# A graph-network kernel: its first block prepared in another order, a shorter lag between its layers, and its last block updated in halves

## Chip, cores, metric

One core of one Trainium2 chip. The metric is device time in microseconds, the median of several executions; before and after were timed on the same chip in the same rounds. Ratios are the mean time of one kernel's fast runs over that of the other's of the same rounds, so not quite the ratio of the medians quoted. "Span" is the length of the one profiled execution; times in traces count from its start. In the rounds of the experiments the kernel before took 653.9 to 655.2 us (medians), 3 to 5 us more than in those of the result, so kernels of different rounds are compared by their ratios or traces.

## The reference, cut

128 graphs of 64 nodes with 128 features. For each pair of nodes a message network runs on the concatenated features; messages are masked by the adjacency matrix, summed over neighbours, and an update network of the same form is added to the features.

```python
def _mlp(x, w0, b0, g0, be0, w1, b1, g1, be1, w2, b2):
    h = jax.nn.relu(x @ w0 + b0)
    h = _layernorm(h, g0, be0)
    h = jax.nn.relu(h @ w1 + b1)
    h = _layernorm(h, g1, be1)
    return h @ w2 + b2

messages = _mlp(pair_feats, msg_w0, ...) * coupling_matrix[..., None]
agg = jnp.sum(messages, axis=2)
updated = part_feats + _mlp(jnp.concatenate([part_feats, agg], -1), upd_w0, ...)
```

## The kernel before

Some names first: two graphs are a pair (128 nodes), two pairs a quad (2560 edge places, five iterations, `QC`), two quads a block. The rows of layer 0 are products of node features and weights; marks and compares build the matrix that picks two rows for each edge. A root is the standard deviation that a layer norm divides by. PSUM is the memory that TensorE writes to; a bank is one buffer of a pool in it, and this kernel's pools have eight.

It lists the edges that exist, 640 places for a graph, and works on 160 iterations of 512 edges. Iteration n runs layer 0 of edges n, layer 1 of edges n - 10, and, on a plan of (iteration, place in it, function), everything else: 16 blocks of 8 graphs are prepared, reduced and updated, one block every ten iterations (`CPB = 10`). Each engine is given its instructions in the order in which the plan emits them, and the traces show them start in that order (under e6_bias a ReLU whose input TensorE ends at 22.00 us starts at 25.12, after the pack of the bias table that the plan puts before it). All eight banks are in use; the update layers, the rows of layer 0 and the derived weights share one (`ps_u`), the transposes two (`ps_a`):

```python
ps_a = es.enter_context(tc.tile_pool(name="ps_a", bufs=2, space=PSUM))
ps_u = es.enter_context(tc.tile_pool(name="ps_u", bufs=1, space=PSUM))
...
def ubank():
    return ps_u.tile([P, 512], F32, name="mu")
...
def layer(b, *pairs):
    ps = ubank()
    ...                       # 8 or 16 passes of TensorE into ps
...
L1 = 2 * QC                   # lag of layer 1: QC = 5
for b in range(NB):
    o = b * CPB
    ...
    u = o + L1 + 3 * QC
    ...
    at(u + 6, "x", lambda b: layer(b, ("xnT", u0a), ("ysumT", W["w2u"])), b)
    at(u + 7, "m", layer_out, b, "uh", "m0")        # DVE empties the bank
    ...
    at(u + 11, "x", lambda b: layer(b, ("uhT", W["u1c"])), b)
    at(u + 12, "m", layer_out, b, "uy", "usdb")     # DVE
    ...
    at(u + 17, "x", lambda b: layer(b, ("uyT", W["u2c"])), b)
    at(u + 18, "m", finish, b)                      # DVE, then the store
...
for n in range(last + 1):
    run(n, "a"); run(n, "m")
    if 0 <= n - L1 < NCHK: layer1(n - L1)
    if n < NCHK: layer0(n)
    ...                       # transposes, statistics, marks and compares
    for k in ("x", "x1", "x2", "e1", "e"):
        run(n, k)
```

A block's first and last update layer stand at u + 6 and u + 17, eleven iterations apart, and the next block's u is ten higher. The last layer of a block therefore runs one iteration after the first layer of the next, whose result DVE has taken by then.

Of the kernel before, what the change touches and what calls it, by code (L numbers as in the profile page):

```python
# [23 lines left out]
def tile_gnn(  # L24
# [74 lines left out]

    an0 = const.tile([P, 2, PB, N], F32, name="an0")  # L100
    xn0 = const.tile([P, 2, PB, C], F32, name="xn0")

    def load_first(b):
        nc.sync.dma_start(an0[:, b], adjp[:, b * PB:(b + 1) * PB, :])
        nc.sync.dma_start(xn0[:, b], xf[b * PB * P:(b + 1) * PB * P, :]
                          .rearrange("(q p) c -> p q c", p=P))

    load_first(0)
    w0a = mat(mw0[0:C, :], "w0a")
    w0b = mat(mw0[C:2 * C, :], "w0b")  # L110
    b0c = col(mb0, "b0c")
    load_first(1)
# [16 lines left out]

    eps_c = const.tile([P, 1], F32, name="eps_c")  # L130
# [3 lines left out]
    nc.scalar.activation(eps2_c, eps_c, AF.Square)  # L134
    first = const.tile([P, PB, N], F32, name="first")
# [5 lines left out]
    lt = const.tile([P, P], F32, name="lt")  # L141
    nc.vector.memset(lt, 1.0)
    nc.gpsimd.affine_select(out=lt, in_=lt, pattern=[[1, P]], compare_op=ALU.is_ge,
                            fill=0.0, base=0, channel_multiplier=-1)
    nc.vector.memset(lt[0:N, N:P], 0.0)

# [3 lines left out]
    nc.vector.memset(dq[N:N + 1, N - 1:N], 0.0)  # L150
# [5 lines left out]
    nc.vector.memset(pick32[0:N, N:N + 1], 0.0)  # L156
    pick = const.tile([P, 2, N], F16, name="pick")
    nc.vector.tensor_copy(pick.rearrange("p g m -> p (g m)"), pick32)
# [4 lines left out]
    cmpt = const.tile([P, 4 * CAP], F16, name="cmpt")  # L163
    ones_row = const.tile([1, P], F32, name="ones_row")
    nc.vector.memset(ones_row, 1.0)
    mean_m = const.tile([P, P], F32, name="mean_m")
    nc.vector.memset(mean_m, 1.0 / C)
# [77 lines left out]
    def square_sum(stp, st, n, name):  # L245

        d = stp.tile([P, n], F32, name=name + "_d")
        s = stp.tile([P, n], F32, name=name + "_s")
        m2 = stp.tile([P, n], F32, name=name)
        nc.gpsimd.tensor_tensor(d, st[:, :, 1], st[:, :, 4], op=ALU.subtract)  # L250
        nc.gpsimd.tensor_tensor(s, st[:, :, 2], st[:, :, 5], op=ALU.add)
        nc.gpsimd.tensor_tensor(d, d, d, op=ALU.mult)
        nc.gpsimd.tensor_scalar(d, d, C / 4.0, None, op0=ALU.mult)
        nc.gpsimd.tensor_tensor(m2, d, s, op=ALU.add)
        return m2
# [7 lines left out]
    def var1_of(stp, st, m20, n, name):  # L263

        v = stp.tile([P, n], F32, name=name + "_v")
        nc.gpsimd.tensor_scalar(v, m20, EPS, None, op0=ALU.mult)
        m2 = square_sum(stp, st, n, name)
        nc.gpsimd.tensor_tensor(v, v, m2, op=ALU.add)
        return v
# [20 lines left out]
    def edge_path(es):  # L290
# [5 lines left out]
        hp = es.enter_context(tc.tile_pool(name="hp", bufs=11))  # L296
        yp = es.enter_context(tc.tile_pool(name="yp", bufs=14))
# [66 lines left out]
        def count_out(b):  # L364
            blk = blocks[b]
            nc.scalar.copy(cumall[:, b * PB:(b + 1) * PB], blk.pop("ps")[:, 0:PB])
            blk["deg"] = blkp.tile([P, PB], F32, name="deg", bufs=5)
            nc.scalar.copy(blk["deg"], blk["rk"][:, :, N - 1])

        def place(b):  # L370

            blk = blocks[b]
            an = blk.pop("an")
# [6 lines left out]
            nc.gpsimd.tensor_tensor(pos, pos, an, op=ALU.mult)  # L380
            blk["pos"] = pos
            qs = qsp.tile([P, PB, 2, P], F16, name="qs")
            nc.gpsimd.tensor_copy(qs[:, :, :, 0:N],
                                  pick.unsqueeze(1).to_broadcast([P, PB, 2, N]))
            nc.gpsimd.memset(qs[N:P, :, 0, N:P], 0.0)
            nc.gpsimd.memset(qs[0:N, :, 1, N:P], 0.0)
            blk["qs"] = qs

            a2 = adp.tile([P, PB, N], F32, name="a2")
            nc.gpsimd.tensor_tensor(a2, an, an, op=ALU.mult)  # L390
            nc.gpsimd.tensor_tensor(a2, a2, an, op=ALU.subtract)
            blk["a2"] = a2
# [19 lines left out]
        def turn(b, src):  # L412
            blk = blocks[b]
            blk[src + "_ps"] = abank()
            for q in range(PB):
                nc.tensor.transpose(blk[src + "_ps"][:, q * P:(q + 1) * P], blk[src][:, q, :],
                                    ident)

        def turn_out(b, src, bufs=1):
            blk = blocks[b]  # L420
            blk[src + "T"] = blkp.tile([P, PB * P], F32, name=src + "T", bufs=bufs)
            nc.scalar.copy(blk[src + "T"], blk.pop(src + "_ps"))
# [77 lines left out]

        def var0_of(q):
            V0[q] = square_sum(stp, ST0.pop(q), QT, "m20")
# [40 lines left out]
        def var1_step(q):  # L543
            Q[q] = var1_of(stp, ST1.pop(q), V0.pop(q), QT, "m21")

        def bias_table():
# [23 lines left out]
            nc.gpsimd.tensor_tensor(W["b1t"], mix[0:K].unsqueeze(1).to_broadcast([K, QT, C]),  # L570
                                    tile_of[0:K].unsqueeze(2).to_broadcast([K, QT, C]),
                                    op=ALU.mult)
# [26 lines left out]
        def weights(p):  # L599
# [3 lines left out]
            for g in range(2):  # L603
                k = (2 * h + g) * TG
                nc.gpsimd.tensor_tensor(  # L605
                    w[:, :, g, :], OH[p][:, :, g, :],
                    Q[q][:, k:k + TG].unsqueeze(2).to_broadcast([P, TG, N]), op=ALU.mult)
# [3 lines left out]
        def reduce(p):  # L611
            b, k = divmod(p, PB)
            if k == 0:
# [13 lines left out]
        def sums_out(b):  # L627
            blocks[b]["ysum"] = updp.tile([P, PB, C], F32, name="ysum")
            nc.scalar.copy(blocks[b]["ysum"], YS.pop(b))

        def bias0(b):
            m0 = updp.tile([P, PB, C], F32, name="m0")
            nc.gpsimd.tensor_tensor(
                m0, bc(W["c2u"], PB),
                blocks[b]["deg"].unsqueeze(2).to_broadcast([P, PB, C]), op=ALU.mult)
            nc.gpsimd.tensor_tensor(m0, m0, bc(W["ub0b"], PB), op=ALU.add)
            blocks[b]["m0"] = m0

        def residual(b):
            xo = updp.tile([P, PB, C], F32, name="xo")  # L640
            nc.gpsimd.tensor_tensor(xo, blocks[b]["xn"], bc(W["cu2b"], PB), op=ALU.add)
            blocks[b]["xo"] = xo

        def layer(b, *pairs):
            ps = ubank()
            for q in range(PB):
                s = slice(q * P, (q + 1) * P)
                for n, (src, w) in enumerate(pairs):
                    nc.tensor.matmul(ps[:, s], lhsT=blocks[b][src][:, s], rhs=w, start=(n == 0),
                                     stop=(n == len(pairs) - 1))  # L650
            blocks[b]["l_ps"] = ps.rearrange("p (q c) -> p q c", q=PB)

        def layer_out(b, o, bias):
            t = updp.tile([P, PB, C], F32, name=o)
            add_relu(t, blocks[b]["l_ps"], blocks[b][bias])
            blocks[b][o] = t
            st = updp.tile([P, PB, 6], F32, name=o + "_st")
            for q in range(PB):
                nc.vector.bn_stats(st[:, q, :], t[:, q, :])
            blocks[b][o + "_st"] = st  # L660

        def upd_m0(b):
            blocks[b]["m2"] = square_sum(updp, blocks[b]["uh_st"], PB, "um0")

        def upd_root0(b):
            blocks[b]["sd"] = root0(updp, blocks[b]["m2"], PB, "um0")

        def upd_shift(b):
            sdb = updp.tile([P, PB, C], F32, name="usdb")
            nc.gpsimd.tensor_tensor(  # L670
                sdb, bc(W["bu1b"], PB),
                blocks[b]["sd"].unsqueeze(2).to_broadcast([P, PB, C]), op=ALU.mult)
            blocks[b]["usdb"] = sdb

        def upd_m1(b):
            blocks[b]["v1"] = var1_of(updp, blocks[b]["uy_st"], blocks[b]["m2"], PB, "um1")

        def upd_root1(b):
            blocks[b]["v1"] = root1(updp, blocks[b]["v1"], PB, "um1")

        def upd_inverse(b):
            blocks[b]["q1"] = inverse(updp, blocks[b]["v1"], PB, "um1")

        def finish(b):
            blk = blocks[b]
            o = updp.tile([P, PB, C], F32, name="uo")
            for q in range(PB):
                nc.vector.scalar_tensor_tensor(o[:, q, :], blk["l_ps"][:, q, :],  # L688
                                               blk["q1"][:, q:q + 1], blk["xo"][:, q, :],
                                               op0=ALU.mult, op1=ALU.add)  # L690
            nc.sync.dma_start(of[b * PB * P:(b + 1) * PB * P, :]
                              .rearrange("(q p) c -> p q c", p=P), o)
            blocks[b] = None
# [6 lines left out]
        L1 = 2 * QC  # L700
        for b in range(NB):
# [4 lines left out]
            if b > 0:  # L706
                r = max(o - 12, 0)
                at(max(o - 13, 0), "m", rank, b)
                at(r, "x", count, b)
                at(r + 1, "a", count_out, b)  # L710
                at(r + 1 if b == 1 else o - 9, "e", place, b)
                at(o - 6, "m", odd_weights, b)
                at(o - 6, "x", steps, b)
                at(o - 5, "a", steps_out, b)
                at(o - 7, "x", turn, b, "xn")
# [296 lines left out]
```

## Time and profile before

| | before |
|---|---|
| time, median of 4 | 650.62 us (650.29 to 653.32) |
| span of the profiled run (an execution of 655.82 us, above the four timed) | 653.6 us |
| TensorE busy, whole span | 624.3 us, 96% |
| TensorE busy, 45.2 to 588.0 us | all of 542.8 us |
| DVE, POOL, ACT busy, whole span | 76%, 58%, 53% |

The prediction shows and reads the lines.

### The profile page before, as it was taken

The page shows a single profiled execution, that of the slowest core. Times are in us where ns is not written, and L with a number is a line of the kernel's source. Part 1 is how long each engine was busy: PE and PEld are TensorE (multiplying, and loading weights), DVE is VectorE, ACT ScalarE, POOL GpSimd, SP SyncE. Part 2 cuts the span into 40 slices and gives each one's busy share as a digit, 9 for nine tenths or more (in the row PEclk, how much of TensorE's full clock was granted, in tenths as well). Part 3 has the DMA queues.
Part 4 walks back from the last instruction along what each step waited for, and adds up shares of the span by engine and source line. Part 5 has one row for each costly group of instructions (what it writes and reads, how often), then busy time and mean ns, then how long its engine had stood idle before and what let it go on. Part 6 is the DMA issues. An engine that isn't in the chain of part 4 may idle for free. (4 is left out here: it accounts for less than half of the span.)

```text
span 653.6 us, 15818 instructions
## 1 busy us (share of the span) xinstructions
PE 624.3 (96%) x5859; PEld 573.4 (88%) x5859; DVE 496.4 (76%) x1871; ACT 349.3 (53%) x788; POOL 377.5 (58%) x956
## 2 busy tenths in 40 slices
PE   4989999999999999999999999999999999999864
PEld 2778999999999999999999999999999999998753
DVE  4778888888777878887777888877787888875332
ACT  2435565665646465665646556565656566464321
POOL 6624446556483846657383855658384765456552
PEclk9979999999999999999999999999999999999985
DMA  4100000001001010101001010100100000000001
GB/s 116 39 1 26 2 25 2 3 1 42 1 3 42 1 42 3 42 2 25 17 3 42 2 43 1 42 2 2 42 1 18 2 18 2 17 3 18 2 17 34
DMA packets 27884, 12.06 MB, mean 18 GB/s; under 512 B 10390, under 2 KB 27804, under 8 KB 27804
## 3 DMA queue, kind: packets, MB, share of 16 engines
q1 hardware_dynamic: 27804, 11.02, 6.4%
q8 instruction: 47, 0.77, 0.5%
q14 instruction: 33, 0.27, 0.1%
HBM read 6.82 MB, written 4.19 MB: 17 GB/s over the span
## 5 line engine op out<-in xcount | busy, mean ns | idle before, releaser
L499 DVE BATCH_NORM_STATS2 st<-hT 128x6 f32<-128x128 f32 x640 | 140.8, 282 | 55.3 <-PE hT L495 55.0
L531 PEld LDWEIGHTS z<-w1c,h 128*128 128x128 f32 x1280 | 168.7, 192 | 7.0
L531 PE MATMUL z<-w1c,h 128*128 128x128 f32 x1280 | 168.9, 275 | 0.0
L541 DVE BATCH_NORM_STATS2 st<-y 128x6 f32<-128x128 f32 x640 | 137.8, 277 | 10.8 <-ACT y L534 10.8
L534 ACT ACTIVATE y<-z 128x512 f32<-128x512 f32 x160 | 95.7, 598 | 87.4 <-PE z L531 86.4
L489 ACT ACTIVATE h<-hps,b0c 128x512 f32<-128x512 f32 x160 | 109.4, 684 | 12.5 <-PE hps L486 12.4
L478 DVE TENSOR_TENSOR s<-mk,cmpt 128x512 fp32r<-128x512 f32 x160 | 107.6, 673 | 4.6 <-POOL cmpt L782 4.0
L495 PE MATMUL hT<-ident,h 128*128 128x128 f32 x640 | 98.1, 276 | 1.7 <-DVE st L499 1.7
L486 PE MATMUL hps<-s,abl 128*128 128x512 f32 (+3 forms) x256 | 93.0, 375 | 0.0
L605 POOL TENSOR_TENSOR w<-oh,m_q 128x320 f32<-128x320 f16 x128 | 89.9, 725 | 3.2 <-PE ma L589 1.0
L495 PEld LDWEIGHTS hT<-ident,h 128*128 128x128 f32 x640 | 76.9, 142 | 12.3 <-DVE st L499 2.4
L596 ACT CAST oh<-ma 128x384 f16<-128x384 f32 (+1 forms) x128 | 48.2, 429 | 61.9 <-PE ma L589 61.1
L528 PE MATMUL z<-b1t,sdT 80*128 80x512 f32 x160 | 78.9, 493 | 1.9 <-ACT y L534 1.9
L620 PE MATMUL ys<-y,w 128*64 128x128 f32 x1280 | 78.2, 275 | 1.0 <-POOL w L605 1.0
L486 PE MATMUL hps<-s,abh 128*128 128x512 f32 (+3 forms) x256 | 79.1, 327 | 0.0
L620 PEld LDWEIGHTS ys<-y,w 128*64 128x64 f32 x1280 | 69.5, 137 | 8.6 <-POOL m_d L250 2.9
L510 POOL TENSOR_TENSOR sh<-m_sd,sh 128x40 fp32r<-128x40 f32 x32 | 8.7, 271 | 116.9 <-ACT sh L509 116.9
L471 PE MATMUL mk<-tp,qs 128*128 128x512 f16 (+3 forms) x256 | 62.2, 305 | 3.9 <-DVE s L478 3.4
L446 DVE TENSOR_TENSOR abl<-mu,abh 128x512 fp32r<-128x512 f32 x32 | 22.1, 691 | 53.2 <-ACT abh L439 53.2
L250 POOL TENSOR_TENSOR m_d<-st 128x20 f32<-128x20 f32 x64 | 16.1, 252 | 79.2 <-DVE st L541 66.9
L486 PEld LDWEIGHTS hps<-s,abl 128*128 128x128 f32 x256 | 49.9, 195 | 0.8 <-issue 0.7
L486 PEld LDWEIGHTS hps<-s,abh 128*128 128x128 f32 x256 | 50.0, 195 | 0.0
(184 smaller groups left out, 1074.8 us busy)
## 6 DMA issues: line engine op xcount, KB each, us to landing
xn<-in_x_dram SPq DMA_DIRECT2D x16, 256.0 KB, 3.5
out_dram<-uo SPq DMA_DIRECT2D x16, 256.0 KB, 2.5
an<-in_adj_dram SPq DMA_DIRECT2D x16, 128.0 KB, 2.6
w<-in_L_gnn_msg_w_dram SPq DMA_DIRECT2D x2, 64.0 KB, 2.7
u<-in_L_gnn_upd_w_dram SPq DMA_DIRECT2D x2, 64.0 KB, 2.1
w0a<-in_L_gnn_msg_w_dram SPq DMA_DIRECT2D x1, 64.0 KB
w0b<-in_L_gnn_msg_w_dram SPq DMA_DIRECT2D x1, 64.0 KB
u0b<-in_L_gnn_upd_w_dram SPq DMA_DIRECT2D x1, 64.0 KB, 1.7
```

What stands on the lines that cost most here:

```text
L471: nc.tensor.matmul(MK[n][:, c:c + w], lhsT=blocks[g // (2 * PB)]["qs"][:, g // 2 % PB, g % 2, :], rhs=TP[g // 2][:, e:e + w], start=True, ...
L478: nc.vector.tensor_tensor(S[n], MK.pop(n), cmpt[:, o:o + CH * P], op=ALU.is_equal)
L486: nc.tensor.matmul(ps[:, c:c + w], lhsT=ab[:, g % 4, :], rhs=s[:, c:c + w], start=(k == 0), stop=(k == 1))
L489: nc.scalar.activation(H[n], ps, AF.Relu, bias=b0c)
L495: nc.tensor.transpose(ps[:, t, :], H[n][:, t * P:(t + 1) * P], ident)
L499: nc.vector.bn_stats(ST0[q][:, CH * c + t, :], ps[:, t, :])
L528: nc.tensor.matmul(ps, lhsT=SD[q], rhs=W["b1t"][:, CH * c:CH * c + CH, :], start=True, stop=False, skip_group_check=True)
L531: nc.tensor.matmul(ps[:, t, :], lhsT=h[:, t * P:(t + 1) * P], rhs=W["w1c"], start=False, stop=True, skip_group_check=True)
L534: nc.scalar.activation(Y[n], ps, AF.Relu)
L541: nc.vector.bn_stats(ST1[q][:, CH * c + t, :], Y[n][:, t, :])
L605: nc.gpsimd.tensor_tensor(w[:, :, g, :], OH[p][:, :, g, :], Q[q][:, k:k + TG].unsqueeze(2).to_broadcast([P, TG, N]), op=ALU.mult)
L620: nc.tensor.matmul(YS[b][g * N:(g + 1) * N, k, :], lhsT=w[:, t, g, :], rhs=y, start=(t == 0), stop=(t == TG - 1))
```

## The change

Its intent: shorten both ends. Four parts, from a long diff:

```diff
 # head: split loads, two weights issued by ACT, TensorE warmed, chain reordered
-    load_first(0)
-    w0a = mat(mw0[0:C, :], "w0a")
+    nc.sync.dma_start(an0[:, 0], adjp[:, 0:PB, :])
+    load_first(0, 0, 2)
+    w0a = mat(mw0[0:C, :], "w0a", nc.scalar)
 ...
+        for n in range(7):
+            nc.tensor.matmul(warm[:, 0:P], lhsT=mean_m, rhs=mean_m, start=True, stop=True)
 ...
-            nc.gpsimd.tensor_tensor(W["b1t"], mix..., tile_of..., op=ALU.mult)
+        def bias_part(c):                              # on ACT, in five packs of four
+            for t in range(CH * c, CH * c + CH):
+                nc.scalar.activation(W["b1t"][:, t, :], W["b1mix"], AF.Copy,
+                                     scale=W["tile_of"][:, t:t + 1])
+        for c in range(QC):
+            at(4 + c, "a", bias_part, c)
 # lag
-        L1 = 2 * QC
+        L1 = QC + 3
+        SC = QC + L1 + QC
 # updates: n is the start of the block's update, one block every ten iterations
-            at(u + 6, "x", lambda b: layer(b, ("xnT", u0a), ("ysumT", W["w2u"])), b)
-            at(u + 17, "x", lambda b: layer(b, ("uyT", W["u2c"])), b)
-            at(u + 18, "m", finish, b)
+                at(n + 3, "x", lambda u: layer(u, ("xn", u0a), ("ysumT", W["w2u"])), u)
+                at(n + 13, "x", lambda u: layer(u, ("uyT", W["u2c"])), u)
+                at(n + 14, "m", finish, u)
 # tail: last block in two halves, its small operations on DVE instead of POOL
+            if b < NB - 1:
+                units = [(Unit(b, 0, PB, nc.gpsimd), o + QC + SC)]
+            else:
+                units = [(Unit(b, 0, 2, nc.vector), o + SC), (Unit(b, 2, 2, nc.vector),
+                                                              o + QC + SC)]
+            return nc.vector if q == NQ - 1 else nc.gpsimd      # last quad's variances
+                (nc.vector if p == NP - 2 else nc.gpsimd).tensor_tensor(   # weights
```

## The prediction

> **What bounds the kernel now.** I read the page's slices first, then the busy time by stretch, then the waits of TensorE alone, then the timelines of the first 60 us and of the last 65 us. The slices say where to look:
>
> ```profile
> PE   4989999999999999999999999999999999999864
> PEclk9979999999999999999999999999999999999985
> ```
>
> TensorE is full except in the first two slices and the last three, and its clock falls only near the third slice and at the end. Busy time by stretch (start and end in us, length, then PE, PEld, DVE, ACT, POOL busy, then the granted clock) shows how sharp that is:
>
> ```profile
> 15.30:20.00 4.70, 4.23 (x24) 2.89 (x23) 2.33 (x4) 0.69 (x1) 2.87 (x7) 1.00 0.71 187
> 33.30:38.10 4.80, 2.65 (x16) 1.62 (x15) 4.80 (x13) 1.12 (x3) 2.81 (x7) 0.96 0.00 0
> 38.10:41.10 3.00, 3.00 (x15) 2.85 (x14) 1.60 (x7) 0.82 (x3) 0.00 (x0) 0.50 0.00 0
> 45.20:588.00 542.80, 542.80 (x5258) 505.24 (x5258) 442.78 (x1688) 315.59 (x711) 317.69 (x819) 1.00 0.06 15
> 588.00:653.60 65.60, 48.71 (x424) 42.59 (x422) 25.13 (x102) 19.13 (x46) 34.73 (x88) 0.83 0.06 17
> ```
>
> From 45.2 to 588.0 us TensorE has no gap at all, with DVE at 82% and POOL at 59%. No part of the change takes work from TensorE, so these 542.8 us cannot shrink; only the head and the tail can. TensorE's own waits (who waited, on whom, us in total, times, longest) lie in those two places too:
>
> ```profile
> PE ma L416 <- DMA xn<-in_x_dram: 4.7, 1, 4.7
> PE mk L471 <- DVE s L478: 3.4, 1, 3.4
> PE mu L649 <- ACT ysumT L422: 2.3, 1, 2.3
> PE hT L495 <- DVE st L499: 1.7, 1, 1.7
> PE ys L620 <- POOL w L605: 1.0, 4, 0.3
> ```
>
> The head's timeline (start, duration) names the causes:
>
> ```profile
> 14.41 0.69 DVE L478 TENSOR_TENSOR s<-mk,cmpt 128x512 fp32r<-128x512 f32 x1 [3.97 <-POOL cmpt L782]
> 15.29 0.88 PE L486 MATMUL hps<-s,abl 128*128 128x512 f32 x1
> 27.25 0.48 PE L486 MATMUL hps<-s,abl 128*128 128x512 f32 x1
> 30.22 4.47 POOL L570 TENSOR_TENSOR b1t<-b1mix,tile_of 80x2560 fp32r<-80x2560 f32 x1
> 32.89 1.99 DVE L455 TENSOR_SCALAR tp<-slot,cumall 128x640 f16<-128x640 f16 x1
> ```
>
> The first compare waits 3.97 us for a table that POOL fills last, so layer 0 starts at 15.29. The same matmul takes 0.88 us there and 0.48 at 27.25: TensorE is at half rate until about 24.2, although the clock column still prints 1.00 (it seems to know no throttle before its first event). Then POOL's bias table holds POOL for 4.47 us; a DVE instruction that takes 0.38 us elsewhere (at 26.02) takes 1.99 beside it and ends with it at 34.9; TensorE stands still, and its clock is 0.50 from 37.8 to 44.6.
>
> The tail's timeline shows a latency chain, not a full engine:
>
> ```profile
> 626.76 1.16 PE L649 MATMUL mu<-u1c,uhT 128*128 128x128 f32 x8
> 632.47 0.80 PE L649 MATMUL mu<-w2u,ysumT 128*128 128x128 f32 x2 [2.35 <-ACT ysumT L422]
> 646.51 2.07 PE L649 MATMUL mu<-u2c,uyT 128*128 128x128 f32 x8 [2.06 <-ACTq L975]
> ```
>
> The last reduction ends at 626.7, and 26.9 us more pass: transposes, three small layers, statistics on POOL and roots on ACT one after another, at half clock from about 632.
>
> [...] 0.88 against 0.48 us, and the fall at 37.8 after the gap of 33.9 to 35.7. [...] TensorE was busy from 18.1 and warm at 24.2. [...] here one issue takes 0.43 to 0.51 us, so moving two weights to ACT is worth about 1 us of issue.
>
> **A ledger of TensorE work at full clock.** From start-to-start times in the full stretch: layer 0 of an iteration 0.55, transposes 0.44, marks 0.25, layer 1 1.20, reduction of two pairs 2.33, node marks 0.25, transposes of a block 0.44, first update layer 1.8, the other two 0.9 each, a half of the rows 1.0. Up to 45.2 us: ten iterations of layer 0 (12.4), rows 3.0, one layer 1 (1.2), preparation and derived weights together about 4.8: 21.4. The head therefore loses 45.2 - 21.4 = 23.8 us. After 588.0: ten layer 1 (12.0), four double reductions (9.3), six node marks (1.5), eight transposes (3.5), layers 5.4 + 2.7 + 3.6, the rest 0.6: 38.6; the tail loses 65.6 - 38.6 = 27.0. Total work 21.4 + 542.8 + 38.6 = 602.8.
>
> **The change part by part: head.** The table is built early and in parts, the step tables are emptied by two engines, the degrees leave the chain, and the placement goes from POOL (0.30 + 0.63 + 0.73) to DVE. New chain: adjacency lands 3.1, scan to 3.8; seven warm-up matmuls, 14 passes of 0.21 us, end about 4.2 and cost the count 0.4; count and copy to 5.0; placement of five DVE instructions to 6.0; meanwhile x's first half turned at 5.5; rows (2.0 us cold) to 7.5; steps to 8.7; copies 0.35, marks 0.6, compare 0.7: layer 0 at about 10.6, against 15.29, so 4.7 earlier. A memset of 1.6 us (three quarters of the 2.19 seen) now sits between the first two compares, so the second iteration starts near 13.5, against 20.0. Iterations 1 and 2 cold at 3.3, iteration 3 with rows 2.5 to 3.5, iteration 4 about 3 (below), 5 to 7 at 2.3, the DVE's load there (0.89 + 0.67 + about 0.7): iteration 8, where layer 1 now starts, comes at 32.5. Work done by then: 15.5. Loss 17.0 in place of 23.8; I take a **gain of 6.4 us**. It includes that the stall behind the bias table, with its cold 7 us, does not come back.
>
> **Lag of 8.** In the full stretch it moves nothing off TensorE. Its worth is at the ends: two iterations fewer with layer 0 alone (where DVE, not TensorE, is the limit), and 7.9 us of work done before layer 0 ends that was done after: two layer 1 (2.4), one double reduction (2.3), two node marks (0.5), the first update layer of one block (1.8) and the last of another (0.9). So 30.7 us of work stays in the tail.
>
> **Tail.** Let T be the end of layer 0. Layer 1 alone is spaced by 2.08 us when nothing fills it (as from 599.77 to 601.85), since one bank of PSUM waits for ACT. Iterations 160 to 167 come to about 20.3 us with one double reduction and the updates between. Reduction of the next pairs and of the last ones, with the last weights split over DVE and POOL and variances on DVE: ends near T + 27. From there the last half's chain: copy 0.4, held about 1 by a root that ACT takes first; turn, copy, first layer with the neighbours' work in the queue to T + 31.5; add, statistics and the small DVE operations (12 of about 0.17 us) 3.5; root 0.3, shift on POOL 0.55, second layer 0.9, add and variance 2.0, root and inverse 0.6, copy and last layer 1.3, finish 0.57, store 3.8 (as 649.8 to 653.6), and about 1.5 for cold matmuls: T + 47. The tail then loses 47 - 30.7 = 16.3 in place of 27.0: a **gain of 10.7 us**.
>
> **Sum.** 6.4 + 10.7 = 17.1 us. Span 653.6 - 17.1 = 636.5; for the time, 650.4 - 17.1 = 633.
>
> **The rivals.** (1) ACT becomes the head's new stop. The bias table is now 20 small activations in four-packs ahead of the ReLU of iterations 4 to 8, and the first pack waits for a POOL chain of 1.7 us after a DVE reduction. In-order ACT then holds the ReLU, and the one bank of layer 0 holds TensorE. I put in 1 us; if it is 3 and the clock drops again, the head gains 2 and the time is 637. For it: ACT sits at its limit nowhere else, but this wait is in program order. (2) The shorter lag exposes the root's chain in every group of five iterations: root, cast, POOL's difference and transpose now stand in one iteration. 0.5 us in each of 32 groups would be 16 us and the time 649. Against it: the transposition is placed last in TensorE's list, behind 0.9 to 3.1 us of update layers, and POOL's weights precede it in another iteration. (3) The halves cost more than they save: small operations have fixed costs (0.16 us for an inverse of 128x4), three units interleave in in-order queues, and tail gains only 4: 640. (4) The warm-up works at once, and the cold stretch of 15 to 24 us goes as well: 3 to 4 us more, 629.
>
> **Range and chances.** (1) and (3) in part are likely, (4) as likely as not, (2) unlikely as a whole. From 626 (both ends better by 3 to 4) to 641 (one rival in full). The line for 2% is 637.4, 4 us above my figure with a spread of about 6: faster 0.77, same 0.22, slower 0.01.
>
> **What would show it.** Right: layer 0's first ReLU at 11 to 13 us instead of 16.63; no gap near 34 and no half clock from 37.8 to 44.6; between the first layer 1 and the end of layer 0 TensorE still without gaps; last reduction's end to the span's end near 20 us instead of 26.9. Wrong: gaps of TensorE that repeat every five iterations, a TensorE wait on ACT in the first 30 us above 2 us, or a chain after the last reduction of over 24 us.

Measured in the trace of before: 0.88 and 0.48 us are the two matmuls above, and the first ten DMA issues take 0.43 to 0.51 us (later ones down to 0.25). The clock column prints 1.00 up to 24.06 us, where the record of the clock begins. For the fixed costs of rival 3: an inverse of 128x4 takes 0.16 us on DVE, one of 128x20, five times as much, 0.26.

## The result

**698.91 us (698.02 to 699.34) against 650.62: ratio 1.0731, interval 1.070 to 1.076.** The change is 7% slower. The span is 696.3 us.

The slices of the changed kernel, to be laid beside those of before:

```profile
PE   6799999899998989989898998989899898989874
PEclk8999999999999999999999999999999999999986
```

The tail looks alike, and the first two slices (6 and 7 in place of 4 and 9) do not tell which head is better; the ruler below does. But the middle, which had no slice under 9, now has an 8 every two or three slices. Busy time by stretch (same columns as in the prediction) says the same:

```profile
100.00:600.00 500.00, 471.70 (x4478) 438.93 (x4477) 369.28 (x1403) 267.45 (x599) 270.79 (x709) 0.97 0.06 15
```

TensorE now stands still for 28.3 of 500 us there, and its granted clock is 0.97. TensorE's waits name one cause (us in total, times, longest):

```profile
PE mu L701 <- DVE uo L737: 34.8, 16, 2.6
PE mu L701 <- ACT uyT L692: 3.6, 2, 2.1
PE ma L538 <- POOL sh L533: 3.2, 4, 1.1
PE hps L505 <- ACT h L508: 2.8, 2, 2.5
PE mk L490 <- DVE s L497: 2.8, 2, 1.9
```

L701 is the update layer and `mu` the bank that `ubank()` hands out; L737 is the finish. Sixteen waits of 2.2 us on average, about one a block. One of them, from the timelines of TensorE and of DVE:

```profile
294.35 1.11 PE L701 MATMUL mu<-u2c,uyT 128*128 128x128 f32 x8
296.67 1.10 DVE L737 SCALAR_TENSOR_TENSOR uo<-mu,um_q,xo 128x128 f32<-128x128 f32 x4
297.82 0.80 PE L701 MATMUL mu<-u0a,xnT 128*128 128x128 f32 x2 [2.36 <-DVE uo L737]
298.41 0.64 PE L701 MATMUL mu<-w2u,ysumT 128*128 128x128 f32 x2
```

The last layer of a block ends at 295.46. The first layer of the next block, in the same iteration, wants the same bank. DVE can empty it only after the rest of its own iteration, at 296.67, and TensorE resumes at 297.82. The last line also shows the second price: the pair takes 0.64 us where it takes 0.39 at full clock (as at 339.56). The granted clock by stretches of 2 us (the third number from the end; the share and rate of DMA follow it) shows how long that lasts:

```profile
296.00:298.00 2.00, 0.18 (x1) 0.18 (x2) 1.77 (x8) 0.00 (x0) 0.08 (x1) 0.93 0.00 0
298.00:300.00 2.00, 2.00 (x10) 2.00 (x11) 0.00 (x0) 0.00 (x0) 0.00 (x0) 0.50 0.63 158
300.00:302.00 2.00, 2.00 (x12) 1.88 (x12) 0.41 (x1) 0.08 (x1) 0.00 (x0) 0.71 0.64 170
302.00:304.00 2.00, 2.00 (x18) 1.95 (x18) 1.15 (x5) 1.76 (x5) 0.65 (x4) 1.00 0.00 0
```

Not every block pays it: after the wait at 336.85 to 339.23 the clock stayed at 1.00. The record of the clock shows a pattern in this. The eight half-clock stretches between 100 and 600 us last 3.41 us each and start whole multiples of 3.41 us apart (174.85, 256.77, 297.73 us and so on). Cut into intervals of the same length, on the same starts, each of them follows an interval in which TensorE stood still for 1.94 to 2.37 us; the four waits that cost no clock left at most 1.84 us in one interval. That holds for 100 to 600 us of this one trace only: after 600 us an interval with 1.91 us of standing still (from 622.00) is followed by full clock, and one with 1.77 us (from 662.96) by half. What decides it is not shown; no run was made to test it.

A ruler for all kernels below is the start of layer 0's ReLU on ACT, of which there is one in each iteration. These numbers come from the timelines (us):

| kernel | iteration 0 | 8 | 28 | 148 | 158 | end of span | 28 to 148 |
|---|---|---|---|---|---|---|---|
| before | 16.63 | 39.45 | 103.31 | 549.08 | 584.52 | 653.6 | 445.8 |
| after | 10.28 | 35.55 | 102.85 | 593.14 | 632.56 | 696.3 | 490.3 |
| e1_later | 10.52 | 36.55 | 103.86 | 550.32 | 589.19 | 644.4 | 446.5 |
| e5_flag | 10.27 | 35.95 | 103.31 | 549.66 | 585.87 | 641.2 | 446.4 |
| e7_all | 12.89 | 34.61 | 101.98 | 548.32 | 584.52 | 639.9 | 446.3 |
| e12_all_again | 10.43 | 32.62 | 100.00 | 546.49 | 582.71 | 638.0 | 446.5 |
| e9_whole | 12.90 | 33.18 | 100.58 | 547.01 | 583.23 | 640.2 | 446.4 |
| e10_pool | 12.91 | 33.14 | 100.51 | 546.96 | 583.19 | 645.6 | 446.5 |
| e11_tailbanks | 10.28 | 32.88 | 100.25 | 546.74 | 582.96 | 636.5 | 446.5 |

From iteration 28 to 148, twelve blocks, the change costs 44.5 us: 3.7 a block, of which about 2.35 is standing still (28.3 us over the twelve waits in 100 to 600 us) and the rest is slower work: for the same 4368 matmuls TensorE is busy 462.0 us, against 446.4 in e1_later below, which fits the stretches at half clock: eight of 3.41 us at 0.50 lose at most 13.7 of these 15.6 us, an estimate.

### The profile page after: what moved, and what is told of

Read it like the earlier page. It is cut to its first block, busy times and chain, and to the rows that moved or that the text cites. A ratio compares the mean times of both kernels' runs of the same rounds, so it can differ in the third digit from the quotient of the medians.

```text
span 696.3 us, 15879 instructions
## 1 busy us (share of the span) xinstructions
PE 636.4 (91%) x5873; PEld 584.2 (84%) x5873; DVE 503.2 (72%) x1917; ACT 359.0 (52%) x814; POOL 361.8 (52%) x932
## 4 chain that ended last, share of the span: by engine, by line
## 5 line engine op out<-in xcount | busy, mean ns | idle before, releaser
L701 PE MATMUL mu<-u0a,xnT 128*128 128x128 f32 x128 | 34.8, 365 | 34.1 <-DVE uo L737 32.6
L701 PEld LDWEIGHTS mu<-u0a,xnT 128*128 128x128 f32 x128 | 26.9, 259 | 37.3 <-DVE uo L737 35.3
L252 POOL TENSOR_TENSOR um_d<-uh_st 128x4 f32<-128x4 f32 x15 | 3.1, 207 | 92.6 <-DVE uh_st L711 92.6
```

Source lines behind the costliest of these rows:

```text
L701: nc.tensor.matmul(ps[:, s], lhsT=l, rhs=w, start=(n == 0), stop=(n == len(pairs) - 1))
```

## The experiments

**Theory A: the bank.** The first layer stands at 3 after a unit's start, the last at 13, and blocks start ten apart: both ask for the one bank in the same iteration. **Theory B: the lag.** The shorter lag exposes the root's chain or makes another engine the bound (rival 2 of the prediction).

### e1_later: the last layer one iteration later

```diff
-                at(n + 13, "x", lambda u: layer(u, ("uyT", W["u2c"])), u)
-                at(n + 14, "m", finish, u)
+                at(n + 14, "x", lambda u: layer(u, ("uyT", W["u2c"])), u)
+                at(n + 15, "m", finish, u)
```

> The changed kernel with the last update layer and the finish of every block one iteration later, nothing else. Theory A (the single PSUM bank that all update layers, rows and derived weights share is asked for by two blocks in one iteration: the last layer of a block stands at 13 after its start, the first layer of the next block at 3 after its own start, and blocks start 10 apart): TensorE's wait on the finish, 34.8 us in 16 times, falls below 4 us, ten iterations take about 36.5 us again instead of 41.5, and the time is 638 to 646. Theory B (the shorter lag exposes the root's chain, or ACT or POOL became the bound): nothing changes by more than 5 us, so 694 to 704.

Measured: 646.81 us against 654.80 of before, ratio 0.990. TensorE in the middle:

```profile
100.00:570.00 470.00, 469.95 (x4610) 439.56 (x4610) 381.72 (x1457) 275.57 (x616) 279.90 (x735) 1.00 0.06 16
```

No idle time, full clock, 446.5 us for twelve blocks as before (445.8). Two numbers undo the whole loss and leave a small gain; the lag of 8 costs next to nothing in the middle. The time is 0.8 us above the range expected.

### e2_otherbank: nothing moved, another bank

```diff
         def layer(u, *pairs):
-            ps = ubank()
+            ps = abank() if pairs[0][0] == "uyT" else ubank()
```

> The changed kernel with every instruction in its place, but the last update layer writes to the pool of two PSUM banks that transposes use, in place of the single bank. Theory A: the wait on the finish goes although nothing moved in the schedule; 638 to 650, the slack for the bank of the transposes being unknown. Theory B, or a theory that the place of the layer in the order is what hurts and not the bank: 694 to 704.

Measured: 651.30 us, ratio 0.996 (0.992 to 1.000). The order of instructions is that of the slow kernel, only the bank differs, and the loss is gone: 1.073 has become 0.996, and iterations 28 to 148 take 451.3 us instead of 490.3. Of the 4.8 us that are left there against e1_later, 2.7 are new small waits on the transposes' banks:

```profile
PE ma L538 <- DVE uo L737: 2.7, 11, 0.2
```

The other 2.1 are busy time and were not traced. So it is the bank and not the place. The time is 1.3 us above the range I had given.

### e3_before_collide: the collision alone, in the kernel before

```diff
-            at(u + 17, "x", lambda b: layer(b, ("uyT", W["u2c"])), b)
-            at(u + 18, "m", finish, b)
+            at(u + 16, "x", lambda b: layer(b, ("uyT", W["u2c"])), b)
+            at(u + 17, "m", finish, b)
```

> The kernel before, with its last update layer and finish one iteration earlier, so that last layer and next block's first layer stand in one iteration there too; none of the change is in it. Theory A: about 2.4 us of wait and 1 to 2 us of slow clock per block for 15 blocks, so 690 to 705 instead of 650. Theory B: 648 to 653.

Measured: 708.61 us against 654.80, ratio 1.0835, slightly more than expected. TensorE's longest wait in total:

```profile
PE mu L649 <- DVE uo L688: 33.8, 15, 2.8
```

The collision alone, without any other part of the change, is enough for the whole loss, with the same signature.

### e4_lag9: the lag

```diff
-        L1 = QC + 3
+        L1 = QC + 4
```

> The changed kernel with a lag of 9 iterations to layer 1 in place of 8. Theory A: 13 and 3 after the start stay ten apart whatever the lag, so the wait stays near 35 us and the time within 688 to 706. Theory B with the lag as the cause: half of the way to the lag of 10 of the kernel before, so 670 to 680.

Measured: 728.98 us, ratio 1.1164: slower still, a miss for both theories. The waits:

```profile
PE mu L701 <- DVE uo L737: 33.6, 16, 2.3
PE ma L538 <- POOL sh L533: 16.0, 30, 1.5
PE ma L421 <- ACT uyT L692: 4.0, 12, 0.3
```

The collision is there as theory A says, in the same size. A second wait has grown: the transpose of the roots (L538) waits for POOL in 30 of 32 groups, 16.0 us instead of 3.2 in the changed kernel. That is rival 2 of the prediction, which at a lag of 8 is covered by update layers that TensorE runs ahead of it in the same iteration, and at 9 is not. It explains 12.8 of some 29 us over the changed kernel (725.5 against 696.3), and the new wait at L421 another 4.0; most of the rest is that TensorE is busy longer (475.7 against 462.0 us from iteration 28 to 148, for the same number of matmuls), and its cause stays open.

### e5_flag: a second collision of the same kind

Moving the last layer put it into the iteration of another user of the bank, the sum of an overflow flag, once: "PE mu L893 <- DVE uo L737: 2.3, 1, 2.3" in the waits of e1_later.

```diff
-        at(NCHK - 3, "x", flag_sum)
+        at(NCHK - 2, "x", flag_sum)      # on e1_later
```

> The kernel of e1_later with the sum of the overflow flag one iteration later. Since e1_later moved the last layer, that sum asks for the same bank in the same iteration as the last layer of block 13, and TensorE waits 2.3 us once on that finish. Theory A (one bank): that wait goes and the time falls by 2 to 4 us against e1_later (646.8), to 643 to 645. Rival (the loss in the last ten iterations is of the end, not of the bank): no change within 1 us.

Measured: 645.14 us against 653.88, ratio 0.988; e1_later had 0.990. The timed difference (1.7 us, 2 to 4 expected) is within the intervals. The trace is clear: iteration 148 to 158 takes 36.2 us instead of 38.9, and the wait is gone.

### e6_bias: the bias table two iterations later

```diff
-            at(4 + c, "a", bias_part, c)
+            at(6 + c, "a", bias_part, c)     # on e1_later
```

> The kernel of e1_later with the five packs of the bias table two iterations later (6 to 10 in place of 4 to 8). Theory (rival 1 of the prediction: ACT, in order, holds the ReLU of iteration 4 behind the first pack, which waits for POOL's table): TensorE's wait of 3.1 us on that ReLU goes, 3 to 5 us faster than e1_later, so 642 to 644. Rival (POOL or DVE set the pace there and ACT's wait only shows it): within 1 us of e1_later.

In the changed kernel ACT waits for POOL with the first pack, and the ReLU stands behind it:

```profile
23.94 1.28 ACT L597 ACTIVATE b1t<-b1mix,tile_of 80x128 fp32r<-80x128 f32 x4 [1.96 <-POOL b1mix L591]
25.12 0.67 ACT L508 ACTIVATE h<-hps,b0c 128x512 f32<-128x512 f32 x1
25.85 0.50 PE L505 MATMUL hps<-s,abl 128*128 128x512 f32 x1 [2.54 <-ACT h L508]
```

Measured: 645.17 us, ratio 0.987. That wait is gone from TensorE's list, and iteration 8 comes at 33.11 us instead of 36.55; of these 3.4 us the span keeps 1.8 (642.6 against 644.4). All of it is still there at iteration 148; 1.0 is lost from there to 158, where the flag's collision is not mended in this run, and 0.6 after it. Rival 1 of the prediction was real; its timed worth, 1.6 us, is under what I expected.

### e7_all and e8_nowarm: the repairs together; one warm-up matmul instead of seven

e7_all joins e5 and e6 and takes a memset of 1.66 us out from between the first two compares (the one of `ones_row` beside it is left out here):

```diff
-    nc.vector.memset(cmpt[0:N, 0:CAP], 1.0)
+    nc.vector.memset(cmpt[0:N, 0:3 * CH * P], 1.0)
 ...
-        nc.vector.memset(cmpt[0:N, CAP:4 * CAP], 1.0)
         marks(1)
         compare(1)
+        nc.vector.memset(cmpt[0:N, 3 * CH * P:4 * CAP], 1.0)
```

e8_nowarm is e7_all with `range(1)` for `range(7)`.

> e5_flag and e6_bias together, and the memset of 1.66 us that stands between the first two compares split: 1536 columns before the scan, the rest behind the second compare. Candidate to beat both kernels: 2 to 4 us from the flag, 3 to 5 from the bias table, 1 to 2 from the memset, so 635 to 641 against 646.8 for e1_later, 2 to 3% faster than the kernel before.

> e7_all with one warm-up matmul in place of seven. If the warm-up is what makes the rows of the first block run at full clock (0.27 us a matmul at 5.96 us in the changed kernel, against 0.42 in the kernel before), those 16 matmuls cost 0.9 us more and the clock stays low to about 18 us: 2 to 4 us slower than e7_all. If the clock falls again anyway near 12 us, as it does in the changed kernel, then under 1.5 us slower.

Measured: e7_all 640.59 us against 653.88, ratio 0.979 (0.977 to 0.982), 6 us better than e1_later; e8_nowarm 640.42, ratio 0.980. The seven matmuls change nothing that can be timed. The traces, one execution a kernel, suggest why: their effect varies. With seven of them the first rows ran at full clock (0.27 us a matmul) in six traces (after, e1, e5, e6, e11, e12) and at half clock (0.42 us) in four (e2, e7, e9, e10); e4's first ReLU at 10.27 us is as early as in the six. e12 and e7 are the same kernel, so the code alone does not decide it. Where the rows ran at full clock, the first ReLU starts at 10.3 to 10.5 us instead of 12.9. By iteration 8 little of that is left: e12 (32.62) is level with e8 (32.68), whose one warm-up left the rows cold, and 0.5 us ahead of e9 and e10, which were cold too; only e7 is 2.0 behind.

### e9_whole, e10_pool, e11_tailbanks, e12_all_again: the tail taken apart

On e7_all: the last block as one unit again; the last quad's variances, last weights and last block's variances on POOL again; the halves in banks of their own; and a control.

```diff
 # e9_whole (cut)                               # e10_pool (cut)
-            if b < NB - 1:                    -  return nc.vector if q == NQ - 1 else nc.gpsimd
+            if b < NB:                        +  return nc.gpsimd     (and the same for weights, units)
 # e11_tailbanks (lines joined)
-            ps = ubank()
+            if u.b < NB - 1:  ps = ubank()
+            elif u.k0 == 0:   ps = ps_h.tile([P, CH * P], F32, name="hps")
+            else:             ps = ps_k.tile([P, CH * P], F32, name="mk")
```

> e7_all with the last block updated as one unit again (small operations still on DVE). If the halves are worth what the prediction put on them, about half of the tail's gain: 3 to 5 us slower than e7_all. Rival 3 of the prediction (three units in in-order queues and one bank eat the gain): within 1.5 us of e7_all, or faster.

> e7_all with the last quad's variances, the last pair's weights and the last block's variances on POOL again, as in the kernel before; halves kept. The operations take 0.16 to 0.18 us on DVE against 0.20 to 0.26 on POOL, and pairs of weights stand one after another on POOL: 3 to 5 us slower than e7_all. If DVE's own queue is what holds the tail: within 1 us.

> e7_all with the two halves of the last block in banks of their own (those of layer 0 and of the marks, idle by then) in place of the one that block 14 and the two halves share. One bank as the cause of what is left of waits in the tail (4.4 us on DVE's finish and additions in e7_all): 2 to 4 us faster than e7_all, so 637 to 639. If the chain of dependent operations sets the end: within 1 us.

> e7_all again, for comparison on the same chip with the three others: a ratio of 0.977 to 0.982 to the kernel before.

| | time, us | ratio to before | from iteration 158 to the end, us |
|---|---|---|---|
| before (same rounds) | 655.18 | 1 | 69.1 |
| e12_all_again | 640.03 | 0.980 | 55.3 |
| e9_whole | 641.10 | 0.978 | 57.0 |
| e10_pool | 648.38 | 0.9905 | 62.4 |
| e11_tailbanks | 638.25 | 0.976 | 53.5 |

The move from POOL to DVE is worth 7.1 us of tail and 8.3 us of time, more than I expected. TensorE's waits of e10_pool after 600 us show where the time goes without it, into copies that ACT makes behind roots that wait for POOL (5.01, 7.25 and 6.57 us in its timeline):

```profile
PE mu L701 <- ACT uhT L692: 5.5, 2, 5.1
PE mu L701 <- ACT uyT L692: 3.3, 1, 3.3
```

The halves are worth 1.7 us in the traces and nothing that the timing can tell apart (intervals 0.974 to 0.981 and 0.975 to 0.984): here rival 3 of the prediction was right. Own banks in the tail give 1.8 us in both views, also within the intervals. e11_tailbanks has the lowest median of all kernels here: 638.25 us, ratio 0.976 (0.972 to 0.981), 2.4% faster than before; whether it is more than 2% the interval leaves open.

## Why the prediction was wrong

**The step that failed is "No part of the change takes work from TensorE, so these 542.8 us cannot shrink; only the head and the tail can", and its companion on the lag, "In the full stretch it moves nothing off TensorE".** That they cannot shrink was right. That they would not grow was assumed, not checked. I checked the in-order queues for each repeated step, but not the buffers: I never listed who holds the single bank `ps_u` in which iteration. The distance between first and last update layer, eleven before and ten after, stood in the diff. The runs put 44.5 us of loss in twelve blocks there; e1 and e2 take it away by moving the layer or by changing the bank, e3 makes it in the kernel before. None of the four rivals named it; rival 2 looked at the right place, a wait that repeats, but at another chain, which the order of TensorE's list does hide at a lag of 8 (e1 shows no such wait in the middle) and does not at 9 (e4).

**The head was put too high.** Its own sum gives 6.8 us (23.8 - 17.0); it took 6.4 and did not say why. To read the gain from a trace, the moved work has to be taken into account. When iteration 158 starts, e5_flag has done two layer 1, a first and a last update layer and nine transposes more than before, by the counts of TensorE's instructions. With their times in the full stretch that is 6.1 us, an estimate. (The prediction's 7.9 also has a double reduction and two node marks; both kernels have done equally many of these by then.) In e5_flag iteration 158 comes 1.35 us later than in before (585.87 against 584.52), so up to there it gained 6.1 - 1.35 = 4.7 us; predicted 6.4. The same count at the end of layer 0 (590.8 against 587.0) gives 8.6 - 3.8, about the same. In the changed kernel layer 0 started at 9.48 us (10.6 predicted), iteration 8 at 33.4 (32.5). The stall on the bias table was put at 1 us and was 2.5, one of the prediction's own signs of being wrong (a wait on ACT above 2 us in the first 30).

**The tail was put too high as well.** From iteration 158 on, before takes 69.1 us, 63.0 without the 6.1 of moved work; e5_flag takes 55.3. The gain is 7.7 us, not 10.7. The chain after the last reduction was even shorter than predicted (17.8 us from 623.45 to 641.2, about 20 said); what was late is the last reduction itself, 32.6 us after the end of layer 0 (590.8) where the prediction had 27. The move to DVE brings 7.1 us and the halves 1.7; together they are 1.1 over the gain, which one trace for each kernel does not resolve.

**Sum.** Head and tail together: 4.7 + 7.7 = 12.4 us, which is 653.6 - 641.2, the span of e5_flag against that of before; 17.1 was predicted. These are single executions, a slow one of before and the fastest of e5_flag: the medians of the same rounds differ by 8.7 us (653.88 - 645.14). The collisions cost the other 55.1 us (696.3 - 641.2): 51.9 in the blocks, 3.2 at the flag once the first was mended (2.7 of it between iterations 148 and 158).

**Warm-up.** It was priced at 0.4 us with a better case of 3 to 4. The first rows were warm in some executions, but of the 2.5 us that this gave at iteration 0 about 0.5 is left at iteration 8 (e12 against e9 and e10; 2.0 against e7).

## What to carry to other kernels

When a software pipeline is shifted, list for every buffer with one copy who writes it and who empties it in each iteration, modulo the period: two uses a whole period apart meet in the next round. A bottleneck engine without any gap is a reason to search a change for what could open one. And in a drained pipeline's last microseconds, look first at which engine the short dependent operations run on (here worth 7.1 us of tail).
